# A sparse four-layer graph network: the first table and the output stored by one 128-partition transfer per unit, x in two arrangements, three adjacency blocks loaded earlier

## The chip, the core and the metric

The kernel runs on one core of a Trainium2 chip. The core has a matrix engine (TensorE, PE in the profile, with its weight loads as PEld), VectorE (DVE), ScalarE (ACT), GpSimd (POOL) and SyncE (SP), which only issues transfers. All engines run at the same time, each executes its own instructions in order, and semaphores make one wait for another. Transfers issued by SP and by POOL are carried out by 16 DMA engines. The metric is device time of one execution in microseconds, as the median of several runs; lower is better.

## The reference

The input x has 8 batches of 2048 nodes with 128 features. The adjacency matrix is 2048 by 2048, symmetric, with ones on its diagonal and a random one in about 0.8% of the other places. Four layers follow each other, attention with eight heads (0 and 2) and graph attention (1 and 3):

```python
# layers 0 and 2
Q = (h @ Wq).reshape(B, N, 8, 16); K = ...; V = ...
scores = jnp.einsum('bnhd,bmhd->bhnm', Q, K) / 4
attn = softmax(jnp.where(adj == 0, -inf, scores), axis=-1)
x = layer_norm(h + (einsum('bhnm,bmhd->bnhd', attn, V).reshape(B, N, 128) @ Wo + bo), ln1_g, ln1_b)
x = layer_norm(x + relu(x @ W1 + b1) @ W2 + b2, ln2_g, ln2_b)
# layers 1 and 3
h = x @ W; s_i = h @ a_src; s_j = h @ a_dst
e = leaky_relu(s_i[:, :, None] + s_j[:, None, :], 0.2)
att = softmax(jnp.where(adj == 0, -inf, e), axis=-1)
x = layer_norm(einsum('bij,bjd->bid', att, h) + x) * ln_gamma + ln_beta
```

## The kernel before

The adjacency is sparse, so the kernel (class `Sparse`) makes lists of neighbours first and then works on gathered rows only. A second class, `Dense`, computes everything without lists; it stands in a branch at the end of `net` that is taken only if a list overflowed, which does not occur here.

**Units.** The nodes are cut into 32 units of 64. A unit's data for all 8 batches stands in one tile of 128 partitions and 512 columns: batches are split into two halves of four, the half and the node within the unit together make 128 columns for each of the four batches of a half. Transposed x of a unit, `xt_dram[u]`, has the 128 features on the partitions; its columns run over batch, half, node.

**Setup.** `run` first calls `load` for every fourth unit: one 1 MB transfer brings four units of transposed x into half of a `kv` buffer that serves as a ring. For each unit `project` (with n = 0) multiplies these columns by Wk and Wv (PE, L1404), copies the results into a tile `trows` (ACT or DVE, L1342 and L1344) and stores them into `table_0`, a table in DRAM with one row of 8 KB per node: 4 KB for half 0 (keys of its four batches, then values) and 4 KB for half 1. A unit's tile is thus 128 partitions of 4 KB. With columns in the order half, node, partitions 0 to 63 hold half 0 and partitions 64 to 127 half 1, and `store` (L1459) issues one transfer for each half. `trows` has two buffers, and the setup also uses the one of `hidden`, so three units' rows can be on their way.

`block_list` handles the adjacency in 16 blocks of 128 nodes: a 1 MB load into a `kv` buffer (L1028), a masking pass on DVE (L1036), the search for the 40 largest (L1054, L1067, L1069), positions by small matmuls (L1090). `unit_list` then makes for each of the block's two units (L1111 to L1195) a list of indices `idx` and a one-hot tile `hot`, which ACT converts to one byte an element (`hot8`) and which goes to DRAM as `hots[u]` (L1199, issued on POOL for the first twelve units, on SP after).

**Attention** (`attention`, n = 0 and 2). For each unit `fetch` loads x (L1257) and the one-hot tile (L1268, widened on ACT at L1275), PE computes queries (L1570). Then in five steps POOL gathers the neighbours' table rows (L1536, an indirect transfer of 128 rows; two in four steps, one in the last), PE spreads the queries to them (L1609), DVE multiplies and sums (L1621, L1628), ACT takes exponents (L1638), POOL weighs the values (L1647), PE adds up (L1679). `after_attention` finishes the unit and calls `project` for the next layer's table. A gather waits for the whole table of its layer. **Graph attention** (`graph`, n = 1 and 3) does the same with rows of 1040 floats, 4160 bytes (L1855 to L1893); in layer 3 each unit's result is stored into `out_dram` by `store` (L1958), again one transfer for each half.

**Order.** No engine's order is written by hand. Every operation is recorded as an `Op` with a cost, a key and its reads and writes; `Plan.order` plays the program through with these costs and, on each engine, takes the operation of the smallest key that is ready and finds its buffers free. `in_order` then fixes that order. A key thus says how early an operation may come: loads of x have u - 1500, the first two adjacency blocks i - 1491, the others 10 i - 80, a unit's step in layer n about 1000 n + 5 u. Buffers of a tag such as `kv` (six) are handed out in the order of keys. All plain transfers of SP share eight completion semaphores in turn, and each waits for the transfer eight before it.

Of the kernel before, what the change touches and what calls it, by code (L numbers as in the profile page):

```python
# [9 lines left out]
F32 = mybir.dt.float32  # L10
# [32 lines left out]
QB = 4  # L43
STRIDE = 1000
LEAD = 60

SBUF_BUFS = {
    "kv": 6, "hot": 3, "hot8": 2, "x": 4, "q_sb": 2, "rows": 3, "at": 1, "r": 2, "x1": 2, "hidden": 1, "normed": 2,
# [18 lines left out]
class Dense:  # L67
# [10 lines left out]
    def __init__(self, ctx, tc, x, adj, w, out):  # L78
        self.tc, self.nc, self.w, self.x_in, self.out = tc, tc.nc, w, x, out
        self.B, self.N, _ = x.shape  # L80
        self.NB = self.N // P
        self.NC = self.N // CH

        def pool(name, **kw):
            return ctx.enter_context(tc.tile_pool(name=name, **kw))

        self.const = pool("const", bufs=1)
        self.dram = pool("dram", bufs=1, space=DRAM)
        self.dram2 = pool("dram2", bufs=2, space=DRAM)
        self.ps_s = pool("ps_s", bufs=2, space=PSUM)  # L90
        self.ps_acc = pool("ps_acc", bufs=1, space=PSUM)
        self.ps_m = pool("ps_m", bufs=1, space=PSUM)

        self.constants()
        self.layers = [
            self.mha_weights(n) if kind is MHA else self.gat_weights(n)
            for n, kind in enumerate(LAYERS)
        ]
        self.masks(adj)

        self.one = pool("one", bufs=1)
        self.two = pool("two", bufs=2)
        self.three = pool("three", bufs=3)
        self.four = pool("four", bufs=4)
        self.kpool = pool("kpool", bufs=9)
        self.vpool = pool("vpool", bufs=5)
        self.turn = 0
# [420 lines left out]
    def batch(self, b):  # L528
        x = self.two.tile([P, self.NB, P], F32, name="x")
        self.nc.sync.dma_start(out=x, in_=self.x_in[b].rearrange("(t p) d -> p t d", p=P))  # L530
        for n, kind in enumerate(LAYERS):
            if kind is MHA:
                units = 2 * self.NB * (self.N // QC)
                gen = self.attention(x, n)
            else:
                units = self.NB * self.NC
                gen = self.graph(x, n)
            for u in gen:
                yield u / units
        self.nc.sync.dma_start(out=self.out[:, b, :].rearrange("(t p) d -> p t d", p=P), in_=x)  # L540

    def run(self):

# [211 lines left out]
def flat(ap):  # L755
    return ap if len(ap.shape) == 2 else ap.rearrange("p b d -> p (b d)")


class Sparse:
# [12 lines left out]

    def __init__(self, ctx, tc, x, xt, adj, w, out):
        self.tc, self.nc, self.w, self.xt_in, self.out = tc, tc.nc, w, xt, out
        self.B, self.N, _ = x.shape
        self.NB = self.N // P
        self.NU = self.N // UNIT
        self.HB = self.B // 2  # L780

        def pool(name, **kw):
            return ctx.enter_context(tc.tile_pool(name=name, **kw))

        self.nc.scalar.preload_act_table_set("natural_log_exp_and_others")
        self.const = pool("const", bufs=1)
        self.dram = pool("dram", bufs=1, space=DRAM)
        self.plan = Plan(self.nc)
        self.op, self.cell = self.plan.op, self.plan.cell
        for tag, bufs in SBUF_BUFS.items():  # L790
            self.plan.pool(tag, pool(f"sb_{tag}", bufs=bufs), bufs, tag in BY_KEY)
        for tag, bufs in PSUM_BUFS.items():
            self.plan.pool(tag, pool(f"ps_{tag}", bufs=bufs, space=PSUM), bufs)

        self.constants()
        self.weights_at = [Cell() for _ in LAYERS]
        self.keys_at = Cell()
        self.late = False
        self.whole()
        self.gates = {}  # L800
# [12 lines left out]

        self.xd = self.dram.tile([self.NU, P, CH], F32, name="xd")
        self.x_at = [Cell() for _ in range(self.NU)]
        self.hots = self.dram.tile([self.NU, P, HOT], F8, name="hots")
        self.hots_at = [Cell() for _ in range(self.NU)]
        self.ends_at = [None] * self.NU
        self.t = self.const.tile([P, self.NU, P // GROUP * self.HB], F32, name="t")
        self.t_at = [Cell() for _ in range(self.NU)]  # L820
        self.idx = self.const.tile([P, self.NU, TILES], I32, name="idx")
        self.idx_at = [Cell() for _ in range(self.NU)]


        self.owner = self.const.tile([P, self.NU, TG, 2], F32, name="owner")
        self.ends = self.const.tile([P, self.NU, 2], F32, name="ends")

        self.empty = self.const.tile([P, self.NU, TILES], F32, name="empty")


        self.seen = self.const.tile([P, 4, self.NB], F32, name="seen")
        self.junk = self.const.tile([P, P], F32, name="junk")
        self.stats = self.const.tile([P, 6], F32, name="stats")
        self.eps = self.fixed("eps", EPS)
        self.half = self.fixed("half", 0.5)
        self.rows_n = self.fixed("rows_n", float(self.N))
        self.huge = self.fixed("huge", 1e30)
# [183 lines left out]
    def block_list(self, adj, i):  # L1021
# [5 lines left out]
            {"SP": 0.45},  # L1027
            lambda e: e.dma_start(out=buf.tile[:, 0:N].bitcast(I32), in_=adj[i * P : (i + 1) * P, :]),  # L1028

            i - 1491 if i < 2 else key - 20,  # L1030
            writes=[buf],
            dma=P * N * 4,
        )
# [189 lines left out]
    def load(self, u, ring):  # L1223

        key = u - 1500
        x = Cell()
        at = u % 8 * CH

        def start(e):
            e.dma_start(  # L1230
                out=ring.tile[:, at : at + 4 * CH].rearrange("p (u c) -> p u c", u=4),
                in_=self.xt_in[u : u + 4].rearrange("u p c -> p u c"),
            )

        self.op({"SP": 0.45}, start, key, reads=[self.gates[u - 9]] if u > 8 else [], writes=[x], shares=[ring], dma=4 * P * CH * 4)
        for k in range(4):
            self.project(
                0, u + k, x, key + k, lambda ring=ring, at=at + k * CH: ring.tile[:, at : at + CH], [ring]
            )
# [144 lines left out]
    def project(self, n, u, x, key, of=None, shares=()):  # L1384
# [68 lines left out]
        if halves[-1] == 0:  # L1453
            return

        def store(e):
            for part, nodes, hf in self.parts(u):
                half = hb * width
                e.dma_start(out=self.tables[n][nodes, hf * half : (hf + 1) * half], in_=rows.tile[part])  # L1459

        self.op(
            {"SP": 0.9}, store, key, reads=[rows], joins=[self.table[n]], dma=P * hb * width * 4
        )

    def norm(self, r, key):
# [439 lines left out]
    def after_graph(self, n, u, outs, banks, acc, x, base):  # L1905
# [36 lines left out]
        if n < len(LAYERS) - 1:  # L1942
            x = self.scaled(normed, L["ln_gamma"], L["ln_beta"], "xnew", key)
            self.keep(u, x, key)
            self.project(n + 1, u, x, key)
        else:

            def last(e):
                shape = [P, len(blocks), P]
                e.tensor_tensor(normed.tile, normed.tile, L["ln_gamma"].unsqueeze(1).to_broadcast(shape), ALU.mult)  # L1950
                e.tensor_tensor(normed.tile, normed.tile, L["ln_beta"].unsqueeze(1).to_broadcast(shape), ALU.add)

            op({"POOL": 2.4, "DVE": 1.2}, last, key, writes=[normed], port=True)

            def store(e):
                for part, nodes, hf in self.parts(u):
                    batches = slice(hf * hb + blocks.start, hf * hb + blocks.stop)
                    e.dma_start(  # L1958
                        out=self.out[nodes, batches, :],
                        in_=normed.tile[part],  # L1960
                    )

            op({"SP": 0.9}, store, key, reads=[normed], dma=P * P * 4 * len(blocks))

# [54 lines left out]
        before[i.engine] = i  # L2019


def net(tc, x, xt, adj, w, out):

    with ExitStack() as ctx:
        s = Sparse(ctx, tc, x, xt, adj, w, out)
        s.run(adj)
        count = s.failed()
        in_order(tc)
        failed = tc.nc.values_load(count, min_val=0, max_val=P, skip_runtime_bounds_check_because="a count of partitions")
    with tc.If(failed > 0):  # L2030
        with ExitStack() as ctx:
            Dense(ctx, tc, x, adj, w, out).run()
# [33 lines left out]
```

The softmax here doesn't subtract the row's maximum and nothing guards it: scores larger than these inputs give would overflow.

## Time and profile before

| what | value |
|---|---|
| three runs | 3027.98, 3045.35, 3050.05 us; median 3045.35 |
| profiled execution | span 3033.2 us (its page gives the span alone), mean granted TensorE clock 0.887 |
| busy share of the span | PE 78%, DVE 76%, POOL 70%, PEld 47%, ACT 46% |
| DMA moved | 1022.93 MB, mean 337 GB/s |
| table 0 stores | from 12.7 us to 131.3 us |
| first gather of layer 0, first multiplication | 135.5 us, 176.6 us |
| last addition of layer 0 (PE, L1679) | 1136.9 us |

The page gives each engine's busy time; the windows view gives the same for a stretch of the span; the timeline shows instructions in order with the idle time ahead of them and what ended it; the waits view sums these. "SPq" stands for SyncE's queue, on which an instruction's length is the time that the issue took. Landings are read from the semaphores that a transfer's 16 parts raise, and packet times from the trace's record of every DMA packet.

### The profile page before, as it was taken

To read this page: it belongs to the slowest core of one execution; us is meant where nothing else is said; L and a number is where in the kernel's file an instruction comes from. 1 tells how busy PE (TensorE), PEld (TensorE's weight loads), DVE (VectorE), ACT (ScalarE), POOL (GpSimd) and SP (SyncE) were. 2 spreads that over 40 slices of the span, in tenths; PEclk is the share of its full clock that TensorE was granted. 3 is DMA by queue.
4 is the path that set the end of the run, shared out by engine and by line. 5 is a ranking of instruction groups with operands and counts; after the bars stand their busy time and mean duration, and the time that the engine had idled before them with its cause. 6 is when DMAs were issued, how large, how long until landed. Compare 5 with 4: busy or idle time off the path is not lost. (4 is left out here: it accounts for less than half of the span.)

```text
span 3033.2 us, 60151 instructions
## 1 busy us (share of the span) xinstructions
PE 2358.7 (78%) x22044; PEld 1417.6 (47%) x22044; DVE 2314.6 (76%) x3754; ACT 1405.2 (46%) x4780; POOL 2135.3 (70%) x1454
## 2 busy tenths in 40 slices
PE   6767887788887776787786778878888878677775
PEld 5633444444443334666664234334334334566664
DVE  4779999998887775555553988888987988566665
ACT  4435555455544442555553235445445434344443
POOL 0158886787888873766663878878878875677774
PEclk8768999999999998989988899999999999778777
DMA  8759997988898884999998989989999986899996
GB/s 272 265 200 363 352 350 293 348 321 327 343 344 338 334 314 152 405 407 402 397 405 292 374 327 358 366 341 356 366 361 353 345 337 229 295 400 403 399 396 257
DMA packets 249535, 1022.93 MB, mean 337 GB/s; under 512 B 40272, under 2 KB 54352, under 8 KB 177328
## 3 DMA queue, kind: packets, MB, share of 16 engines
q0 software_dynamic: 166464, 864.44, 73.1%
q1 hardware_dynamic: 82768, 154.56, 14.4%
q8 instruction: 177, 2.90, 0.4%
q14 instruction: 126, 1.03, 0.1%
HBM read 978.59 MB, written 88.08 MB: 352 GB/s over the span
## 5 line engine op out<-in xcount | busy, mean ns | idle before, releaser
L1536 POOL DMA_INDIRECT kv<-table,idx x1152 | 1192.8, 1035 | 645.9 <-issue 291.7
L1647 POOL TENSOR_TENSOR kv<-kv 128x2048 f32<-128x2048 f32 (+1 forms) x259 | 929.4, 3602 | 86.5 <-ACT kv L1638 82.7
L1621 DVE TENSOR_TENSOR kv<-qe,kv 128x2048 f32<-128x2048 f32 (+1 forms) x320 | 662.7, 2071 | 156.2 <-DMA kv<-table,idx 116.6
L1628 DVE TENSOR_REDUCE s<-kv 128x128 f32<-128x2048 f32 (+1 forms) x320 | 660.0, 2062 | 8.1 <-ACT junk L1473 0.5
L1609 PE MATMUL qe<-q_sb,hot 32*128 32x512 f32 (+1 forms) x2304 | 397.2, 693 | 207.5 <-DVE kv L1621 202.0
L1679 PE MATMUL acc<-kv,hot 128*32 128x512 f32 (+1 forms) x2304 | 362.3, 643 | 42.1 <-POOL kv L1647 31.9
L1893 PE MATMUL acc_q<-kv,w 128*32 128x129 f32 (+1 forms) x4608 | 220.1, 326 | 141.6 <-DVE w L1877 113.3
L1609 PEld LDWEIGHTS qe<-q_sb,hot 32*128 32x128 f32 (+1 forms) x2304 | 106.0, 195 | 330.4 <-DVE kv L1621 275.6
L1877 DVE TENSOR_TENSOR w<-hot,e 128x512 f32<-128x512 f32 (+1 forms) x384 | 221.2, 598 | 48.9 <-ACT e L1867 47.7
L1893 PEld LDWEIGHTS acc_q<-kv,w 128*32 128x32 f32 (+1 forms) x4608 | 170.6, 134 | 182.0 <-DVE w L1877 111.2
L1638 ACT ACTIVATE kv<-s 128x128 f32<-128x128 f32 (+1 forms) x320 | 95.0, 297 | 323.1 <-DVE s L1628 172.9
L1855 DVE TENSOR_TENSOR e<-te,kv 128x16 f32<-128x16 f32 (+1 forms) x320 | 58.8, 184 | 237.7 <-DMA kv<-table,idx 234.6
L1473 ACT ACTIVATE junk<-ps_c 128x128 f32<-128x128 f32 x492 | 136.0, 277 | 176.2 <-PE ps_c L1366 151.2
L1342 ACT COPY trows<-ps_p 128x258 f32<-128x258 f32 (+1 forms) x230 | 108.2, 473 | 188.3 <-PE ps_p L1406 93.5
L1867 ACT ACTIVATE e<-e 128x16 f32<-128x16 f32 (+1 forms) x320 | 67.1, 212 | 256.4 <-DVE e L1862 253.4
L1679 PEld LDWEIGHTS sums<-kv,hot 128*32 128x32 f32 (+1 forms) x2304 | 88.6, 118 | 207.3 <-issue 205.1
L1893 PE MATMUL acc<-kv,w 128*32 128x129 f32 (+1 forms) x2304 | 118.8, 307 | 75.2 <-DVE w L1877 69.3
L1366 PE MATMUL ps_c<-centre,r 128*128 128x128 f32 x1008 | 147.6, 291 | 29.7 <-DVE r L1729 18.6
L1376 PE MATMUL ps_f<-x,W 128*128 128x512 f32 (+1 forms) x256 | 151.4, 675 | 17.6 <-ACT x L1516 9.7
L1366 PEld LDWEIGHTS ps_c<-centre,r 128*128 128x128 f32 x1008 | 126.9, 197 | 69.8 <-DVE r L1729 37.0
L1679 PEld LDWEIGHTS acc<-kv,hot 128*32 128x32 f32 (+1 forms) x2304 | 55.1, 114 | 197.2 <-issue 108.6
L1759 PE MATMUL ps_y<-hidden,W 128*128 128x512 f32 (+1 forms) x256 | 142.8, 645 | 4.6 <-ACT hidden L1749 3.0
(205 smaller groups left out, 4028.7 us busy)
## 6 DMA issues: line engine op xcount, KB each, us to landing
table<-trows SPq DMA_DIRECT2D x128, 256.0 KB
x<-xd SPq DMA_DIRECT2D x96, 256.0 KB
xd<-xnew SPq DMA_DIRECT2D x93, 256.0 KB
kv<-table,idx POOLq DMA_INDIRECT x1152
table<-trows SPq DMA_DIRECT2D x128, 130.0 KB
kv<-adj_dram SPq DMA_DIRECT2D x16, 1024.0 KB
kv<-xt_dram SPq DMA_DIRECT2D x8, 1024.0 KB
x<-xt_dram SPq DMA_DIRECT2D x32, 256.0 KB
```

The lines of the kernel that those rows point to most:

```text
L1366: e.matmul(ps.tile[:, cols], lhsT=flat(x.tile)[:, cols], rhs=self.centre, start=True, stop=True)
L1376: lambda e: e.matmul(ps.tile, lhsT=w, rhs=x.tile, start=True, stop=True),
L1473: e.activation(self.junk, x, AF.Square, scale=P**-0.5, accum_out=var.tile[:, b, 1:2])
L1536: e.indirect_dma_start(out=rows(kv.tile, j), out_offset=None, in_=self.tables[n], in_offset=bass.IndirectOffsetOnAxis(ap=self.idx[:, u, co ...
L1609: e.matmul(qe.tile[:, j, hf, :], lhsT=hot.tile[rows, t * P : (t + 1) * P], rhs=q.tile[rows, :], start=True, stop=True,)
L1621: e.tensor_tensor(k, qe.tile[:, 0:tiles].rearrange("p j h c -> p (j h) c"), k, ALU.mult)
L1628: e.tensor_reduce(s.tile[:, 0 : tiles * heads].rearrange("p (q c) -> p q c", q=2 * tiles), k, axis=mybir.AxisListType.X, op=ALU.add,)
L1647: e.tensor_tensor(v, v, w.unsqueeze(3).to_broadcast([P, 2 * tiles, heads // 2, HD]), ALU.mult)
L1679: e.matmul(out[rows, :], lhsT=hot.tile[:, col : col + GROUP * (3 - tiles)], rhs=rhs[:, 2 * j + hf, :], start=(t == 0), stop=(t == TG - 1),)
L1759: lambda e, f=f, ps=ps: e.matmul(ps.tile, lhsT=L["W2"][:, f, :], rhs=hidden.tile[:, f, :], start=(f == 0), stop=(f == FFN // P - 1),),
L1877: e.tensor_tensor(w.tile[:, :, j : j + tiles, :].rearrange("p x j c -> p j x c"), oh[:, j : j + tiles].unsqueeze(2).to_broadcast(shape), e ...
L1893: e.matmul(acc(b)[at : at + GROUP * (3 - tiles), :], lhsT=w.tile[:, hf * hb + b, j : j + 3 - tiles, :].rearrange("p j c -> p (j c)"), rhs= ...
```

## The change

Table 0 and the output get a layout in which a unit's 128 partitions are 128 consecutive rows. For the table this needs a different order of the projected columns, node before half, so that partition 2 t + h holds half h of node t; x is therefore handed over a second time, as `xk_dram`, in this order, and `load` reads it from there. `fetch` still reads `xt_dram`. `out_dram` becomes an array of units, partitions and columns, which the host puts in order. In layer 0 `store` issues one transfer of 128 partitions, and the output likewise; tables 1 to 3 keep two. In the fallback class the output is stored in two parts. The recorded SP cost of these stores goes from 0.9 to 0.45. The first five adjacency blocks get keys of their own.

```diff
+ADJ = (-1499, -1495, -1487, -1479, -1471)
@@ block_list
-            i - 1491 if i < 2 else key - 20,
+            ADJ[i] if i < len(ADJ) else key - 20,
@@ load
-                in_=self.xt_in[u : u + 4].rearrange("u p c -> p u c"),
+                in_=self.xk_in[u : u + 4].rearrange("u p c -> p u c"),
@@ project
+        half = hb * width
+
         def store(e):
+            if n == 0:
+                by_half = self.tables[0].rearrange("n (h c) -> (n h) c", h=2)
+                e.dma_start(out=by_half[u * P : (u + 1) * P, :], in_=rows.tile)
+                return
             for part, nodes, hf in self.parts(u):
-                half = hb * width
                 e.dma_start(out=self.tables[n][nodes, hf * half : (hf + 1) * half], in_=rows.tile[part])
 
         self.op(
-            {"SP": 0.9}, store, key, reads=[rows], joins=[self.table[n]], dma=P * hb * width * 4
+            {"SP": 0.9 if n else 0.45}, store, key, reads=[rows], joins=[self.table[n]], dma=P * half * 4
         )
@@ after_graph
-            def store(e):
-                for part, nodes, hf in self.parts(u):
-                    batches = slice(hf * hb + blocks.start, hf * hb + blocks.stop)
-                    e.dma_start(
-                        out=self.out[nodes, batches, :],
-                        in_=normed.tile[part],
-                    )
-
-            op({"SP": 0.9}, store, key, reads=[normed], dma=P * P * 4 * len(blocks))
+            op(
+                {"SP": 0.45},
+                lambda e: e.dma_start(out=self.out[u][:, cols], in_=flat(normed.tile)),
+                key,
+                reads=[normed],
+                dma=P * P * 4 * len(blocks),
+            )
@@ kernel
-    xt = x.reshape(2, b // 2, n_nodes // UNIT, UNIT, P).transpose(2, 4, 1, 0, 3).reshape(n_nodes // UNIT, P, b * UNIT)
+    parts = x.reshape(2, b // 2, n_nodes // UNIT, UNIT, P)
+    xt = parts.transpose(2, 4, 1, 0, 3).reshape(n_nodes // UNIT, P, b * UNIT)
+    xk = parts.transpose(2, 4, 1, 3, 0).reshape(n_nodes // UNIT, P, b * UNIT)
...
-    out = nc.dram_tensor("out_dram", [n_nodes, b, P], F32, kind="ExternalOutput").ap()
+    out = nc.dram_tensor("out_dram", [n_nodes // UNIT, P, b * UNIT], F32, kind="ExternalOutput").ap()
```

More of the change, by code (lines that the diff above doesn't have):

```diff
@@ L539, in batch @@
                 yield u / units
-        self.nc.sync.dma_start(out=self.out[:, b, :].rearrange("(t p) d -> p t d", p=P), in_=x)
+        halves = P // UNIT
+        out = self.out.rearrange("(t v) (h i) (c d) -> v h c i t d", v=halves, i=UNIT, d=P)
+        for v in range(halves):
+            self.nc.sync.dma_start(
+                out=out[v, b // (self.B // 2), b % (self.B // 2)], in_=x[v * UNIT : (v + 1) * UNIT]
+            )
     def run(self):
@@ L759, with __init__ @@
 class Sparse:
-    def __init__(self, ctx, tc, x, xt, adj, w, out):
-        self.tc, self.nc, self.w, self.xt_in, self.out = tc, tc.nc, w, xt, out
+    def __init__(self, ctx, tc, x, xt, xk, adj, w, out):
+        self.tc, self.nc, self.w, self.xt_in, self.xk_in, self.out = tc, tc.nc, w, xt, xk, out
         self.B, self.N, _ = x.shape
@@ L1953, in after_graph @@
             op({"POOL": 2.4, "DVE": 1.2}, last, key, writes=[normed], port=True)
-            def store(e):
-                for part, nodes, hf in self.parts(u):
-                    batches = slice(hf * hb + blocks.start, hf * hb + blocks.stop)
-                    e.dma_start(
-                        out=self.out[nodes, batches, :],
-                        in_=normed.tile[part],
-                    )
-            op({"SP": 0.9}, store, key, reads=[normed], dma=P * P * 4 * len(blocks))
+            op(
[4 more added lines that the diff above has]
+                dma=P * P * 4 * len(blocks),
+            )
     def run(self, adj):
@@ L2019, in in_order, with net @@
         before[i.engine] = i
-def net(tc, x, xt, adj, w, out):
+def net(tc, x, xt, xk, adj, w, out):
     with ExitStack() as ctx:
-        s = Sparse(ctx, tc, x, xt, adj, w, out)
+        s = Sparse(ctx, tc, x, xt, xk, adj, w, out)
         s.run(adj)
@@ L2050 @@
     b, n_nodes, _ = x.shape
-    xt = x.reshape(2, b // 2, n_nodes // UNIT, UNIT, P).transpose(2, 4, 1, 0, 3).reshape(n_nodes // UNIT, P, b * UNIT)
-    args = [give("x_dram", x), give("xt_dram", xt), give("adj_dram", np.roll(np.asarray(inputs["adj"]), (-FIRST, -FIRST), axis=(0, 1)))]
+    parts = x.reshape(2, b // 2, n_nodes // UNIT, UNIT, P)
+    xt = parts.transpose(2, 4, 1, 0, 3).reshape(n_nodes // UNIT, P, b * UNIT)
+    xk = parts.transpose(2, 4, 1, 3, 0).reshape(n_nodes // UNIT, P, b * UNIT)
+    args = [give("x_dram", x), give("xt_dram", xt), give("xk_dram", xk), give("adj_dram", np.roll(np.asarray(inputs["adj"]), (-FIRST, -FIRST), axis=(0, 1)))]
     weights = []
@@ L2064 @@
     r = run_bass_kernel_spmd(nc, [arrays], core_ids=[0])
-    return np.roll(r.results[0]["out_dram"].transpose(1, 0, 2), FIRST, axis=1)
+    y = r.results[0]["out_dram"].reshape(n_nodes // UNIT, 2, UNIT, b // 2, P)
+    return np.roll(y.transpose(1, 3, 0, 2, 4).reshape(b, n_nodes, P), FIRST, axis=1)
```

## The prediction

> **What bounds the kernel now.** I read the busy shares by stage first (one row per stretch of the trace: its length, then busy time of PE, weight loads, DVE, ACT and POOL with instruction counts, granted TensorE clock, DMA share, GB/s):
> ```profile
> 0.00:134.00 134.00, 99.77 (x421) 82.19 (x421) 78.51 (x262) 57.31 (x136) 9.69 (x37) 0.82 0.82 269
> 134.00:176.00 42.00, 26.32 (x116) 24.22 (x116) 25.69 (x97) 20.21 (x61) 15.46 (x15) 0.50 0.71 282
> 176.00:250.00 74.00, 55.11 (x334) 25.56 (x334) 67.89 (x78) 24.79 (x64) 55.40 (x30) 0.73 0.61 230
> 250.00:1100.00 850.00, 694.19 (x4834) 348.24 (x4826) 753.77 (x819) 430.10 (x1412) 691.60 (x375) 0.93 0.88 334
> 1300.00:1500.00 200.00, 158.69 (x2470) 128.40 (x2470) 105.59 (x368) 107.43 (x378) 131.53 (x129) 0.89 1.02 402
> ```
> From 176 us on layer 0 keeps DVE busy (67.9 of 74, then 753.8 of 850). Layer 1 keeps the DMA engines full (1.02). The first 176 us are full on nothing: DVE has 55 us idle before 134 and 16 between 134 and 176. The change's main edits lie there. So the timeline of this stretch comes next, then its waits:
> ```profile
> 113.75 18.20 SPq L1459 DMA_DIRECT2D table<-trows  x14
> ...
> 135.53 3.10 POOL L1536 DMA_INDIRECT kv<-table,idx  x1 [8.69 <-issue]
> ...
> 148.99 0.62 POOL L1199 DMA_DIRECT2D hots<-hot  x1
> ...
> 165.16 1.00 ACT L1195 ACTIVATE hot<-hot 128x960 fp8e5<-128x960 f32 x1 [4.16 <-DMA hots<-hot]
> ...
> 173.39 1.00 ACT L1275 CAST hot<-hot 128x960 f32<-128x960 fp8e5 x1
> ...
> 174.45 2.09 PE L1609 MATMUL qe<-q_sb,hot 32*128 32x512 f32 x8 [2.56 <-ACT hot L1275]
> ...
> 176.61 2.29 DVE L1621 TENSOR_TENSOR kv<-qe,kv 128x2048 f32<-128x2048 f32 x1 [3.06 <-PE qe L1609]
> ```
> The last store of table 0 is issued at 131.3 and lands at 134.4 by its semaphore; at 135.5 the first gather of it goes out. The first multiplication of layer 0 comes only at 176.6: it waited for a matmul, that for unit 0's one-hot tile (cast at 173.4), and that for a load behind stores of `hots`:
> ```profile
> SPq L1268 <- DMA hots<-hot: 33.4, 1, 33.4
> ```
> is the SP queue's longest single wait before 300 us. Before 134 us the copies into `trows` waited for earlier stores to land (total, times, longest):
> ```profile
> ACT trows L1342 <- DMA table<-trows: 13.8, 7, 4.1
> ...
> DVE trows L1344 <- DMA table<-trows: 12.8, 2, 7.7
> ```
>
> [...] among stores alone (100 to 134 us) the 4 KB packets split into about 160 and 307 to 382 ns, mean 230; in layer 1, among gathers, such packets take 161. [...] A pair issued at 118.3 and 118.9 begins to land at 121.0 and 121.8. [...] The `hots` store of 148.99, behind nine gathers on POOL's queue, held ACT until 165.16. [...] The row 134 to 176 shows 0.50; ten list matmuls (L1145) take 2.43 us there and 1.24 at 56 us (clock 0.92).
>
> **The change, part by part.** "First multiply" is the 176.6 us above; the order of instructions is read from the two built programs.
>
> *Stores of table 0.* 64 SP issues of 256 KB (0.45 to 0.60 us each) become 32 of 512 KB. A unit's rows come free when both halves have landed, about 0.65 us earlier without the second issue; nine waits x 0.65 = 6 us. The packets, 1408, 1278 and 1410 of them in the three stretches to 134 us at 195, 193 and 230 ns, would take 160: 190 us over 16 engines, 12 us of DMA time. DMA is not full here (0.82), so I take little of that: last landing -7 us, bounds 0 and -18 (6 + 12).
>
> *x in a second arrangement.* The same eight 1 MB loads; later fetches of x still read the old one. 0.
>
> *Adjacency earlier.* Both programs load eight blocks before attention begins; three move from 61 to 80 us to between the x loads. Each is 1 MB, 128 packets of 8 KB at about 350 ns: 2.8 us of the rings. Two of them now stand ahead of the second and third x load. Those landed at 9.5 and 12.2, and would land near 12.3 and 17.8; PE is busy with the first four units until about 17.3, so this is hidden, and if projections caught up it would cost 3 us. DVE gets about 16 us more list work before the last projection (85 against 69, counted by durations), into its 55 us idle. On PE the lists of two more units (about 2.4 us each) and not one query product (2.07) stand before the last projection: +2.7 us on the last landing.
>
> *Hand-over.* Between last projection and first query spread PE had three blocks' offsets, seven unit selections and the parts of five units; now one, two and two, and a query. At half clock: 3.3 + 2 x 0.65 + 2.07 + 2 x 2.9 + 2.1 for the spread = 14.6 us. Alongside, the gathers: 1.1 to the first issue, 4.4 for two, some 5 for 2 MB, 10.5. The first load of unit 0's one-hot tile now waits only for `hots` stores that stand ahead of every gather on POOL, so the 33 us wait goes. First multiply 16 us after the last landing, where it was 42.2; bounds 11 (gathers alone) and 30. What is late next is PE's list work at half clock.
>
> *What is deferred.* At the first multiply nine units' lists are done, not eleven. Two x 2.33 us of DVE (L1167 to L1179) come in layer 0, where DVE is full: +4.7. Eight `trows` copies move from DVE to ACT (8 x 0.69 us), in a stretch where DVE idles: 0. On SP the ninth adjacency load now stands between the one-hot loads of units 0 and 1 and waits for the first gather's buffer. Unit 1's tile is queued behind it and then loads beside gathers; unit 0's five steps (about 21 us) cover most: +3, bounds 0 and 8.
>
> *Output.* 62 stores of 128 KB become 31 of 256, the last four become two. Packets stay 2 KB (84 ns) and bytes are equal, so layer 3's full DMA gains nothing; SP waits there for DVE, so 31 issues saved hide. At the end SP reads the count at 3019.68, 0.3 us after the others, but PE's branch lasts until 3024.4: 0.
>
> *Rest of layer 0.* The same instructions in another order (one row weighting moves from DVE to POOL); from layer 1 on PE, DVE, ACT and POOL have an identical order. 0, bounds -8 and +8.
>
> Sum: last landing 134.4 - 7 + 2.7 = 130; first multiply 146, 30.6 earlier; + 4.7 + 3 = **-23 us**. Against the profiled span of 3033.2 that is 3010. The page gives no time around the span; the three runs are 3027.98, 3045.35 and 3050.05, so their median is 12 us above it and 5 below their highest. I subtract from the median: **3022**.
>
> **The rivals.**
> *The start stays late.* The stores free nothing, because PE (99.8 of 134 busy at clock 0.82) sets the last landing, and first multiply comes 30 us after it, since the lists drag at half clock. 134.4 + 2.7 + 30 = 167, 9.5 earlier; + 4.7 + 3 leaves -2: 3043. For it: PE is the busiest engine before 134. Against: the gaps behind store landings.
> *The stores were the bound.* All 18 us come through: 134.4 - 18 + 2.7 + 16 = 135, 41.5 earlier; + 7.7 gives -34: 3011. For it: 26.6 us of waits on landings, DMA at 0.82; against: SP often waits for ACT's copies (38.7 us before 300), not for DMA.
> *Slower: layer 0's new order.* Where DVE is full (176 to 1100), the remaining eight blocks' list work falls at other places between multiplications. If it comes before a multiplication whose successor on PE or POOL then starves, each unit pays; 1 us a unit is +32, less the 23: 3055. It decides from 0.75 us a unit. For it: DVE idles only 96 of 850 us, PE and POOL are at 82%. Against: the amount of work is equal.
> That the change is not in the program is excluded by the built order.
>
> **Numbers.** Forecast 0.5, start stays late 0.2, stores the bound 0.2, slower 0.1. The forecast's bounds, all at one end at once, would give 2995 or 3059; as independent (root of the squares: 11, 5, 3, 8 below; 7, 3, 14, 5, 8 above) they give 3007 to 3041, its own range. The favourable rival with layer 0's -8 gives 3003, and measurement adds some 10 either way (runs of before spread 22). Range 2990 to 3050, leaving out most of the slower case and the outer tails. One per cent, 30 us, is about what this measurement can tell from no change. Faster by more (below 3015): 0.15 from the forecast's lower part, 0.15 from the second rival, 0.02 else = 0.32. Slower by more (above 3076): 0.06 from layer 0's order at nearly 2 us a unit. Within: 0.62.
>
> **What would show it.** Stores: 32 issues for table 0, their 4 KB packets near 160 ns, copy waits on landings well under 26 us. Last landing at 125 to 133 us; after 140 the stores step is wrong. First multiply at 140 to 152 with no long SP wait on a `hots` store; near 165 the hand-over step is wrong. Layer 0's last multiplication and everything after should shift by one constant; a growing shift is the third rival. The tail after the last DVE instruction stays near 14 us.

## The result, and the profile after

The changed kernel takes 3027.34 us (median of 20 runs, 3010.68 to 3037.61), the kernel before 3033.82 us beside it (20 runs, 3023.67 to 3050.05). Where the two were timed in turn the ratio is 0.9965, 95% interval 0.9947 to 0.9982: about 10.6 us faster, between 5 and 16. The forecast was 23 us, a ratio of 0.9924, which lies outside that interval. That the forecast 3022 lies near the measured number has another reason: it was taken off 3045.35, the median of three runs, and that of twenty is 11.5 us lower. So the direction was right and the gain about half.

The profiled execution of the changed kernel is the longest of its 20 runs (3037.61 us, a span of 3035.9, clock 0.882); before had a span of 3033.2. Spans of single executions say little here; stages do, and even these only where several executions agree. The busy shares by stage, with the columns of the prediction:

```profile
0.00:134.00 134.00, 104.99 (x454) 86.29 (x454) 92.05 (x329) 71.53 (x170) 12.92 (x41) 0.82 0.75 273
134.00:176.00 42.00, 36.20 (x207) 23.84 (x206) 30.98 (x37) 18.02 (x53) 28.86 (x20) 0.61 0.88 349
176.00:250.00 74.00, 52.44 (x346) 25.77 (x347) 63.33 (x79) 29.56 (x93) 55.94 (x32) 0.84 0.80 301
250.00:1100.00 850.00, 694.57 (x4694) 349.75 (x4693) 731.74 (x802) 419.39 (x1379) 677.96 (x365) 0.91 0.86 325
```

In the setup DVE is busier (92.1 us against 78.5), and from 134 to 176 us POOL works 28.9 us against 15.5: layer 0 is already running. But from 176 to 250 us DVE works 63.3 against 67.9, and from 250 to 1100 us 731.7 against 753.8. What was won early is lost in the two lower rows, on the engine that is fullest there.

The timeline of the hand-over, all engines, changed kernel:

```profile
111.86 15.40 SPq L1467 DMA_DIRECT2D table<-trows  x7
...
130.84 1.08 POOL L1547 DMA_INDIRECT kv<-table,idx  x1 [13.49 <-DVE cand L1075]
...
134.64 0.99 ACT L1281 CAST hot<-hot 128x960 f32<-128x960 fp8e5 x1
...
138.87 2.09 PE L1620 MATMUL qe<-q_sb,hot 32*128 32x512 f32 x8
...
141.03 2.29 DVE L1632 TENSOR_TENSOR kv<-qe,kv 128x2048 f32<-128x2048 f32 x1 [0.87 <-PE qe L1620]
```

The last store of table 0 lands at 129.7 by its semaphore (before 134.4), the first gather goes out at 130.84 (135.53), unit 0's one-hot tile is cast at 134.6 (173.4), and the first multiplication comes at 141.0 (176.6): 35.6 us earlier. SP's waits before 300 us (total, times, longest):

```profile
SPq L1034 <- DMA kv<-table,idx: 23.3, 2, 12.9
...
SPq L1274 <- DMA hots<-hot: 14.3, 2, 13.7
```

The wait of 33.4 us ahead of unit 0's one-hot tile is gone; the 13.7 us for `hots` come later, ahead of the third one-hot load (172.3 us). New is a wait of the ninth adjacency load for a gather's buffer. The copies' wait for landed stores before 140 us:

```profile
ACT trows L1348 <- DMA table<-trows: 16.7, 5, 5.5
```

That is all of it now; before it was 13.8 on ACT and 12.8 on DVE. The 4 KB packets of the stores take 164, 182 and 168 ns in the three stretches up to 134 us (195, 193 and 230 before; the forecast's 160 for all of them was an estimate from the shorter ones of before), and 32 issues do what 64 did.

Then the waits of DVE from 180 to 1130 us, first before, then after:

```profile
DVE kv L1621 <- DMA kv<-table,idx: 48.8, 36, 3.7
DVE kv L1621 <- PE qe L1609: 10.7, 10, 1.9
...
DVE r L1729 <- PE ps_o L1376: 7.3, 1, 7.3
```

```profile
DVE kv L1632 <- DMA kv<-table,idx: 42.5, 24, 5.1
DVE kv L1632 <- PE qe L1620: 25.9, 16, 9.1
DVE r L1740 <- PE ps_o L1382: 16.3, 7, 7.2
```

DVE waits less for gathers and more for PE: 15 us more for spread queries, 9 more for the output projection. In all these two come to 25.9 and 16.3 us here; E2 and E12, which have this order too, have 19.4 and 16.8, and 15.1 and 18.4. Layer 0 from its first multiplication to its last took 970.8 us before and 1004.6 in this execution; of the lead of 35.6 us 1.7 were left at its end.

### The profile page after: what moved, and what is told of

It is laid out like the page before. It is cut to its first block, busy times and chain, and to the rows that moved or that the text cites. A ratio compares the mean times of both kernels' runs of the same rounds, so it can differ in the third digit from the quotient of the medians.

```text
span 3035.9 us, 60069 instructions
## 1 busy us (share of the span) xinstructions
PE 2383.0 (78%) x22044; PEld 1429.6 (47%) x22044; DVE 2306.6 (76%) x3744; ACT 1409.6 (46%) x4789; POOL 2139.0 (70%) x1455
## 5 line engine op out<-in xcount | busy, mean ns | idle before, releaser
L1690 PE MATMUL acc<-kv,hot 128*32 128x512 f32 (+1 forms) x2304 | 372.6, 660 | 60.0 <-POOL kv L1658 43.9
L1904 PEld LDWEIGHTS acc_q<-kv,w 128*32 128x32 f32 (+1 forms) x4608 | 171.5, 135 | 172.3 <-DVE w L1888 100.1
L1484 ACT ACTIVATE junk<-ps_c 128x128 f32<-128x128 f32 x492 | 136.1, 277 | 162.8 <-PE ps_c L1372 137.0
L1348 ACT COPY trows<-ps_p 128x512 f32<-128x512 f32 (+1 forms) x238 | 113.3, 478 | 190.1 <-PE ps_p L1412 102.0
L1372 PE MATMUL ps_c<-centre,r 128*128 128x128 f32 x1008 | 150.8, 295 | 28.8 <-DVE r L1740 18.4
L1372 PEld LDWEIGHTS ps_c<-centre,r 128*128 128x128 f32 x1008 | 130.1, 201 | 73.2 <-DVE r L1740 36.7
```

The lines of the kernel that those rows point to most:

```text
L1372: e.matmul(ps.tile[:, cols], lhsT=flat(x.tile)[:, cols], rhs=self.centre, start=True, stop=True)
L1484: e.activation(self.junk, x, AF.Square, scale=P**-0.5, accum_out=var.tile[:, b, 1:2])
L1690: e.matmul(out[rows, :], lhsT=hot.tile[:, col : col + GROUP * (3 - tiles)], rhs=rhs[:, 2 * j + hf, :], start=(t == 0), stop=(t == TG - 1),)
L1904: e.matmul(acc(b)[at : at + GROUP * (3 - tiles), :], lhsT=w.tile[:, hf * hb + b, j : j + 3 - tiles, :].rearrange("p j c -> p (j c)"), rhs= ...
```

## Experiments

Every kernel's order of instructions could be fixed apart from its transfers, so the change splits cleanly: stores (with x twice), output, and order (adjacency keys with the recorded cost). The times of the stages, from one profiled execution each, in us; "layer 0" runs from its first multiplication (L1621) to its last, "rest" from there to the end of the span; the ratio is to the kernel before, with its interval.

| kernel | first gather | first mult. | last mult. | layer 0 | rest | ratio |
|---|---|---|---|---|---|---|
| before | 135.5 | 176.6 | 1147.4 | 970.8 | 1885.8 | 1 |
| the change | 130.8 | 141.0 | 1145.7 | 1004.6 | 1890.2 | 0.9965 [0.9947, 0.9982] |
| E1 stores, old order | 121.2 | 161.6 | 1129.5 | 967.8 | 1877.5 | 0.9973 [0.9959, 0.9987] |
| E2 order, old stores | 135.1 | 144.7 | 1141.1 | 996.4 | 1876.6 | 0.9999 [0.9986, 1.0012] |
| E3 output alone | 136.1 | 177.2 | 1143.4 | 966.2 | 1876.9 | 0.9987 [0.9966, 1.0008] |
| E4 change without output | 131.1 | 141.3 | 1132.8 | 991.5 | 1886.7 | 0.9960 [0.9946, 0.9975] |
| E5 E1, one-hot stores on SP | 129.1 | 169.5 | 1148.1 | 978.7 | 1879.3 | 0.9966 [0.9950, 0.9981] |
| E6 before, one-hot stores on SP | 132.8 | 172.6 | 1155.9 | 983.2 | 1887.2 | 0.9999 [0.9977, 1.0020] |
| E7 E4, one load moved | 130.1 | 140.3 | 1123.4 | 983.1 | 1892.5 | 0.9969 [0.9953, 0.9985] |
| E8 E4, one-hot stores on SP | 129.3 | 139.6 | 1137.9 | 998.3 | 1888.0 | 0.9967 [0.9950, 0.9983] |
| E9 E4, second gather late | 132.6 | 158.6 | 1153.7 | 995.0 | 1894.6 | 1.0024 [1.0006, 1.0043] |
| E10 stores and cost | 118.6 | 157.2 | 1153.7 | 996.5 | 1893.8 | 1.0028 [1.0012, 1.0043] |
| E11 stores and output, old order | 126.4 | 166.9 | 1137.2 | 970.3 | 1886.1 | 0.9966 [0.9949, 0.9982] |
| E12 the change again | 130.9 | 141.1 | 1133.0 | 991.9 | 1887.4 | 0.9973 [0.9955, 0.9991] |

One thousandth of the ratio is 3 us.

### E1: the stores alone

```diff
-                in_=self.xt_in[u : u + 4].rearrange("u p c -> p u c"),
+                in_=self.xk_in[u : u + 4].rearrange("u p c -> p u c"),
...
+            if n == 0:
+                by_half = self.tables[0].rearrange("n (h c) -> (n h) c", h=2)
+                e.dma_start(out=by_half[u * P : (u + 1) * P, :], in_=rows.tile)
+                return
```

> Only the transfers of table 0 change: x in the second arrangement, one 128-partition store a unit; keys and recorded costs are those of before, so that every engine has the order of before. The output is as before. FORECAST (store packets gain, hand-over gains separately): last landing of table 0 about 7 us earlier, near 127; the one-hot tile of unit 0 is still late behind stores of hots on POOL's queue, so the first multiplication moves by no more than those 7 us (168 to 172); total -3 to -8 us, ratio 0.997 to 0.999. If STORES WERE THE BOUND: last landing near 116 to 118, total -15 or more. If LAYER 0 ABSORBS any earlier start: first multiplication 168 to 172 all the same, the shift gone by the end of layer 0, total 0 +-3.

8 us faster (4 to 12). The profiled execution is the shortest of its 22 runs (3008.70 us, median 3022.28). In it the last store lands at 120.1, 14.3 us earlier, which is more than forecast; the first multiplication comes 15.0 earlier, still 40 us after the gather. So the stores shorten the setup and do nothing for the hand-over. Whether the shorter packets or the halved number of issues does it was not separated. Nothing is absorbed: the shift is 15.0 at layer 0's first multiplication and 17.9 at its last. DVE's waits on PE in layer 0 (180 to 1130 us) stay small:

```profile
DVE kv L1626 <- PE qe L1614: 9.0, 10, 1.7
...
DVE r L1734 <- PE ps_o L1376: 2.3, 2, 2.1
```

### E2: the order alone

```diff
-            i - 1491 if i < 2 else key - 20,
+            ADJ[i] if i < len(ADJ) else key - 20,
...
-            {"SP": 0.9}, store, key, reads=[rows], joins=[self.table[n]], dma=P * hb * width * 4
+            {"SP": 0.9 if n else 0.45}, store, key, reads=[rows], joins=[self.table[n]], dma=P * hb * width * 4
```

> Only the order of the change: adjacency keys and recorded SP cost 0.45 for table 0, so that PE, DVE, ACT and POOL have the order of the changed kernel; the stores stay two of 64 partitions, x and the output as before. FORECAST with GIVING BACK IN LAYER 0: first multiplication 5 to 8 us later than in the changed kernel, at 146 to 150 (hand-over gains about 28), then a shrinking lead in layer 0 as in the changed kernel, nothing left at its end or a loss; total -5 to +5. If the ORDER ALONE makes the gain: -8 to -11 as the changed kernel, ratio 0.996. If the slower rival (layer 0's new order) holds in full: +5 or more.

No gain (-4 to +4 us), although the first multiplication comes 31.9 us earlier. The last store lands at 133.8 (before 134.4), so three more blocks among the loads of x cost nothing there. Layer 0 takes 996.4 us where it took 970.8, and 25.6 of the 31.9 us are gone at its end. The hand-over's gain and layer 0's loss both come with these two lines, the adjacency keys and the cost; E10 takes them apart.

### E3 and E4: the output

```diff
             def store(e):
-                for part, nodes, hf in self.parts(u):
...
+                e.dma_start(out=self.out[u][:, cols], in_=flat(normed.tile))
```

> Only the output: one 128-partition transfer a unit and block of columns into the new layout, recorded cost left at 0.9, so that every engine has the order of before. FORECAST: 0 +-2, layers 0 to 2 unchanged, the tail after the last DVE instruction near 14 us. If the OUTPUT makes the gain (fewer issues on SP[...]): -6 to -11 us, all of it in layer 3 and the tail.

E4 is the changed kernel with the old `store` of the output put back.

> The change without its output edit: table 0 by one store a unit, x twice, costs and adjacency keys; PE, DVE, ACT and POOL have the order of the changed kernel. FORECAST: same as the changed kernel within 2 us, ratio 0.996 to 0.997, first multiplication near 141, the lead shrinking through layer 0 in the same units as in the changed kernel's trace (if it is the order that stalls) or in other units (if it is the variation of one execution). If the OUTPUT makes the gain: within 2 us of before.

The output alone gives -10 to +2 us, which decides nothing; but the change without it (-12, interval -16 to -8) is not measurably slower than the change. So the output is no part of the gain that can be seen; a gain of a few us is not excluded. E4's lead in layer 0 shrinks from 35.3 to 14.6 us in the same units as in the change: unit 0's stretch, from its first multiplication to unit 1's, takes 33.8 and 33.6 us (before 25.6), unit 5's 35.9 and 36.7 (28.2), unit 12's 45.9 and 45.9 (34.7); unit 10's, shorter in both, 29.0 and 29.0 (40.6, but 36.6 to 40.6 among the executions with the old order). It is the order, not the execution.

### E5 and E6: the one-hot stores off POOL's queue

```diff
-            lambda e: e.dma_start(out=self.hots[u], in_=hot8.tile),
+            lambda e: (self.nc.sync if 6 <= u < LEAD // TG else e).dma_start(out=self.hots[u], in_=hot8.tile),
```

> E1 (table 0 by one store a unit, order of before) with one thing more: the one-hot stores of units 6 to 11 are issued by SP in place of POOL, so that they no longer stand behind the gathers on POOL's queue. PE, DVE and ACT keep the order of before, POOL too but for these six issues. First gather near 121 as in E1, first multiplication near 142 to 148 (in E1 161.6), about where the changed kernel has it. If it is LAYER 0'S NEW ORDER that gives the lead back (my theory): here the order is the old one, the lead of some 30 us at the first multiplication is still there at layer 0's last (shift -25 to -35), total -20 to -30, ratio 0.990 to 0.993. If LAYER 0 ABSORBS an earlier start whatever its order (gathers, throttle): the lead shrinks to about -15 by its end, total as E1, -8 +-4.

> The kernel before with only the one-hot stores of units 6 to 11 on SP in place of POOL; two stores a unit, old x, keys, costs. First gather at 135 as before, first multiplication near 156 to 162 (before 176.6). LAYER 0'S NEW ORDER as the loser: lead of 15 to 20 us carried to the end of layer 0, total -12 to -20, ratio 0.993 to 0.996. LAYER 0 ABSORBS: 0 to -5.

E5 has the edits of E1 as well, E6 no others. They were to bring the early start without the new order, and didn't: the first multiplication comes at 169.5 and 172.6, 40 us after the first gather as before. In E5 SP's longest wait is now for ACT (before 300 us):

```profile
SPq L1199 <- ACT hot L1195: 86.1, 9, 32.3
```

ACT's timeline shows why:

```profile
138.01 1.01 ACT L1195 ACTIVATE hot<-hot 128x960 fp8e5<-128x960 f32 x1
...
141.00 1.01 ACT L1195 ACTIVATE hot<-hot 128x960 fp8e5<-128x960 f32 x1
...
166.28 1.01 ACT L1275 CAST hot<-hot 128x960 f32<-128x960 fp8e5 x1
```

In the old order the seventh and eighth list are converted 10 and 13 us after the last landing, whatever queue carries their stores: here at 138 and 141 us (landing 128.0), in E1 at 130 and 133 (landing 120.1). SP stands at the first of these stores until 139, with the load of unit 0's tile behind it; the load goes at 150.0, and its cast stands behind one more conversion on ACT, at 165.4. The queue was one link of that chain; taking it out showed the next. E5's total is that of E1. Whether the old order of layer 0 would keep a lead of 30 us was not tried in another way.

E5 shows something else. Up to the last store it has the order of E1, and E11 has it too, but the last store lands at 120.1 in E1, 125.3 in E11 and 128.0 in E5. The stretch from 40 to 50 us, E1 and then E5:

```profile
40.00:50.00 10.00, 9.68 (x48) 8.21 (x48) 4.15 (x8) 4.15 (x11) 0.75 (x1) 0.83 0.82 294
```

```profile
40.00:50.00 10.00, 9.62 (x35) 8.69 (x36) 3.60 (x8) 2.75 (x7) 0.00 (x0) 0.51 0.61 210
```

PE is busy for the whole stretch in both, but at a clock of 0.83 it finishes 48 matmuls and at 0.51 only 35. Just ahead a copy on ACT had waited 0.38 us for a store's landing in E1 and 1.91 in E5. In E11 it waited 1.97, and the clock of the stretch is 0.55. That the longer gap let the clock fall is a guess; no run tested it alone. One execution thus sizes the setup to no better than 8 us.

### E7 and E8: what lengthens unit 0

E7 holds back one transfer:

```diff
+            if i == 8:
+                self.late = go      # the ninth adjacency load
+            else:
+                go()
...
-                lambda e: e.dma_start(out=hot8.tile, in_=self.hots[u]),
+                lambda e: (e.dma_start(out=hot8.tile, in_=self.hots[u]), self.late() if n == 0 and u == 1 else None),
```

> E4 (the change without its output edit) with one transfer moved on SP: the ninth adjacency load goes behind the one-hot load of unit 1 in place of ahead of it; everything else has the order of E4. In E4 unit 0's stretch (first multiplication of unit 0 to that of unit 1) takes 33.8 us, before 25.6. If THIS SP ROW costs what the stretch grew by: stretch 26 to 29, total 5 to 8 us below E4. If the DEFERRED LISTS cost it (PE's list matmuls ahead of the query spread, ACT waiting for a one-hot store behind gathers): stretch 32 to 34, total within 3 us of E4.

E8 is E4 with the edit of E5, from unit 8 on.

> E4 with the one-hot stores of units 8 to 11 issued by SP in place of POOL. In E4 ACT waits 4.5 us at 166.6 for such a store behind gathers, and the cast of unit 1's tile stands behind that. On SP the stores of units 8 and 9 now stand ahead of the ninth adjacency load. If that wait on ACT is what lengthens unit 0: stretch 26 to 30 in place of 33.8, total -4 to -8 below E4. If the DEFERRED LISTS themselves (DVE and PE time, order of PE) do: stretch 32 to 34, and the losses of later units (5, 12, 17) as in E4; total within 3 us of E4, well above E5.

With the load moved, unit 0's stretch is 33.1 us (E4 33.8) and the total no lower than E4's: the SP row costs nothing that can be seen. (In its one profile E7 has a layer 0 of 983.1 us, 8 below E4's; the totals don't show such a gain.) E8 makes the stretch longer (37.2) and the total no lower. That leaves the work itself that now lies in unit 0. In E4 its timeline shows how it counts:

```profile
150.08 2.27 PE L1146 MATMUL ps_l<-unit_aux,hot 128*128 128x86 f32 x10
...
152.14 0.49 PE L1153 MATMUL ps_l<-unit_aux,hot 128*128 128x1 f32 x2
...
152.56 2.09 PE L1615 MATMUL qe<-q_sb,hot 32*128 32x512 f32 x8
152.67 0.57 DVE L1168 TENSOR_TENSOR pick<-rank,ps_l 128x400 f32<-128x400 f16 x1 [1.45 <-PE ps_l L1153]
...
154.72 2.29 DVE L1627 TENSOR_TENSOR kv<-qe,kv 128x2048 f32<-128x2048 f32 x1 [0.87 <-PE qe L1615]
...
159.32 0.29 DVE L986 COPY Wt<-ps_w 128x128 f32<-128x128 f32 x1 [1.37 <-PE ps_w L985]
...
162.73 0.16 DVE L998 COPY Wx<-ps_wa 128x1 f32<-128x1 f32 x1 [0.93 <-PE ps_wa L989]
```

DVE pays for a list not only with its own passes. PE's selections stand ahead of the query spread that the next multiplication needs, so DVE waits 1.45 us for them, and 0.87 for the spread behind them. A second list in the same unit costs 2.51 us of waiting at 171.9. And not only lists were deferred: the last two lines prepare a weight of the next layer (`Wt`, `Wx`), for which DVE waits 1.37 and 0.93 us. In the old order this lies ahead of the first multiplication (at 134 and 150 us in the kernel before), where DVE does not wait for it; the prediction has no term for it.

### E9: has layer 0 a pace of its own?

```diff
             for j in range(tiles):
                 col = 2 * t + j
+                if n == 0 and u == 0 and col == 1:
+                    for _ in range(10):
+                        e.memset(rows(kv.tile, 1), 0.0)
```

> E4 (the change without its output edit) with ten clears of 128x2048 words on POOL between the first and the second gather of layer 0, some 19 us by the 1.85 us of a 128x2048 pass on POOL at the start of the trace before; every engine keeps the order of E4. The first multiplication moves from 141 to some 160, where E1 has it. If LAYER 0 HAS A PACE OF ITS OWN that takes up an earlier or later start: its last multiplication moves by less than 8 us and the total by 0 to +8 against E4 (ratio to before 0.996 to 0.999). If its NEW ORDER loses the time and the start is carried through (my theory): the last multiplication 15 to 20 us later than in E4, total +15 to +20 against E4, slower than before by 3 to 10 us.

POOL's timeline has the delay where it was put:

```profile
132.60 1.07 POOL L1545 DMA_INDIRECT kv<-table,idx  x1 [13.49 <-DVE cand L1070]
133.67 18.58 POOL L1544 MEMSET kv<- 128x2048 f32 x10
152.52 1.03 POOL L1545 DMA_INDIRECT kv<-table,idx  x1 [0.27 <-POOL kv L1544]
```

Against E4 the first multiplication is 17.3 us later, that of unit 10 17.8, of unit 22 17.7, the last 20.9; the total rises from 0.9960 to 1.0024, some 19 us (by the two intervals 12 to 27). A start of layer 0 counts in full. The rival that it takes up any shift is out, and so is the thought that the loss is something that an early start brings about: with a late start and the same order it is the same.

### E10: a third order

Table 0's one store and the recorded cost, with the old adjacency keys.

> Table 0 by one store a unit with its recorded SP cost of 0.45, adjacency keys of before: a third order, which neither the kernel before nor the changed one has. It too leaves one unit's list more to layer 0 (ten done ahead of the first multiplication of DVE's order, against eleven before and ten in the change). If DEFERRED LISTS cost layer 0 its time: layer 0 from its first to its last multiplication 985 to 1000 us as in the changed kernel (983 to 1005), against 971 before, total near before. If the loss belongs to the PARTICULAR ORDER that the adjacency keys give: 965 to 985, total -8 to -15.

Layer 0 takes 996.5 us again and the kernel is 8 us slower than before, though its first multiplication comes 19.5 us earlier. Here it is another wait that grew most (24.4 us on ACT's copies of layer 1's rows, 6.8 before). So the loss does not need the adjacency keys: two orders that leave a list more to layer 0 lose some 27 us each against the old one's 969. (Ahead of the first multiplication DVE has eleven lists done in the old order, ten in E10, and in the change nine and the first two passes of a tenth.) The early hand-over does need the keys: in E10 the first multiplication comes 39.7 us after the last landing (117.5), about as late as before (42.2). The keys with the old cost, which might have the one without the other, were not run. For the total I had expected a draw with the kernel before. With two such orders the number of lists and the placement of the rest can't be told apart.

### E11 and E12: the change without its order, and the change

E11 joins the edits of E1 and E3.

> The change without its reordering: table 0 and the output by one store a unit, x twice, but recorded cost 0.9 and the adjacency keys of before, so that every engine has the order of before. If the transfers make the whole gain: -8 to -13, the same as the changed kernel beside it within 4 us. If the ORDER adds to it: the changed kernel is 4 us or more below this one. If the OUTPUT gains too: this one is 3 to 4 us below E1, -11 to -13.

> The changed kernel once more, beside E11 on the same chip. -8 to -13 against before. Its profile: first multiplication within 2 us of 141, the stretches of units 0, 5, 12 and 17 again 4 us or more above those of before (the losses are of the order, not of one execution); a last multiplication of layer 0 at 1145.7 again would make the first profile typical, one near 1130 an execution that lost more than most.

E11 and the change are the same within their intervals (0.9966 and 0.9973). The reordering brings nothing in sum. E12's profile has the first multiplication at 141.1, unit 0 at 33.8, unit 5 at 38.1, unit 12 at 44.8 and unit 17 at 39.4 us (31.4 before), and the last at 1133.0: the first profile of the change lost more than most. No version was measurably better than the change; E4, the lowest, overlaps it.

E11 and E12 have the same transfers and differ in the order alone. Layer 0 in E11 and then in E12, from the first multiplication to the last, with the columns of the prediction (DVE's is the third busy time):

```profile
166.88:1137.21 970.33, 785.47 (x5424) 393.71 (x5428) 863.95 (x930) 476.49 (x1552) 776.88 (x420) 0.92 0.85 324
```

```profile
141.14:1133.02 991.88, 797.09 (x5429) 401.52 (x5430) 863.21 (x943) 480.50 (x1566) 791.93 (x427) 0.91 0.86 326
```

DVE works as long in both (864.0 and 863.2 us), and the 21.6 us between them are idle time. They are lost by the start of unit 20 (E12 is 23.6 us longer up to there), in whose stretch the last list is finished in both; after that nothing more is lost. So the loss falls where lists are still placed between the units. Not every wait is behind list work, though. The longest one in E12:

```profile
723.65 0.99 ACT L1281 CAST hot<-hot 128x960 f32<-128x960 fp8e5 x1 [5.34 <-DMA hot<-hots]
...
726.01 0.58 ACT L1348 COPY at<-ps_t 128x512 f32<-128x512 f32 x1
...
728.25 2.07 PE L1382 MATMUL ps_o<-at,Wo 128*128 128x512 f32 x2
...
730.36 0.75 DVE L1740 SCALAR_TENSOR_TENSOR r<-ps_o,bo,x 128x512 f32<-128x512 f32 x1 [7.90 <-PE ps_o L1382]
```

DVE waits 7.90 us for an output projection whose input `at` ACT copies only at 726.0, because ACT had stood 5.34 us for a one-hot load. PE runs no list work in this time.

## Why the prediction was right in direction and more than twice too large

*Stores of table 0, -7 on the last landing.* Right within its bounds (0 to -18): 6.4, 9.1 and 14.3 us in three executions of the old order, 4.1 in the new (E2 to the change: 133.8 to 129.7). The old stores vary too: 131.7 us in E6, 134.9 in E3. In total they give 8 us (E1), which is nearly the whole gain.

*Adjacency earlier, +2.7.* Between nothing (E2, 133.8 against 134.4) and 10 us (129.7 in the change against 120.1 to 128.0 with the stores alone). The sum of this term and the last, 130, was measured as 129.7 (128.2 to 131.4 in the other executions with both edits); that doesn't confirm the two terms one by one.

*Hand-over, 16 us after the last landing.* 11.3, at the favourable bound, so that the first multiplication came at 141.0 and not 146. The reason given was only half of it: the `hots` stores behind gathers on POOL's queue were not what set the late start alone. E5 took them off that queue and the start stayed late; it needed the order that the adjacency keys give (E2; E10 without them starts late).

*What is deferred, +4.7 on DVE and +3 on SP, and the rest of layer 0 at 0, within 8.* Here the prediction failed, in size. The four executions with the old order on every engine (before, E1, E3, E11) have layer 0 at 966.2 to 970.8 us, mean 968.8; the five with the new one and no transfer moved (the change, E2, E4, E9, E12) at 991.5 to 1004.6, mean 995.9. The terms together are +27, not +7.7. The executions that moved transfers are less far apart: E5 and E6 have 978.7 and 983.2 with the old order on PE, DVE and ACT, E7 and E8 983.1 and 998.3 with the new; with them the means differ by 22.

Of the 27 us DVE works 2.6 (860.8 us in the mean of the four, 863.4 of the five), less than the 4.7 for the deferred lists, and the SP row is nothing (E7). The other 24.5 are idle time of DVE, for which the prediction had only the term of 0: it took the other blocks' work as neutral because its amount is equal. Its place isn't: one unit gains 11.6 us (unit 10), another loses 11.2 (unit 12). In unit 0 the traces show the idle time behind PE's selections and behind a weight that is prepared there; at the longest wait, behind a late one-hot load on ACT. How the rest divides was not shown.

The clock is a rival that no run sets apart. Over layer 0 the granted TensorE clock is 0.92 in the four and 0.90 to 0.91 in the five, and a slower PE may have lengthened DVE's waits, or the waits have lowered the clock; neither was shown. It is not the whole: unit 0 has 0.63 before and 0.61 in the change, and 25.6 and 33.6 us; unit 16 has 0.98 and 0.74, and 33.3 and 32.6 us.

With the measured terms the sum comes out: 35.6 us at the first multiplication less 27 leaves 8 to 9; the two measurements of the change give 10.6 and 8.2. The parts from layer 1 on range over 10 us among the six executions with the old order and over 18 among the seven with the new, with means of 1882 and 1888; a loss of a few us there is not excluded. *Output, 0*: nothing seen. *Tail near 14 us*: 13.9 after DVE's last instruction.

*The rivals.* "The start stays late" and "the stores were the bound" are both refuted, by 141.0 and by 129.7. "Slower: layer 0's new order" named the right place. It had PE or POOL starve behind DVE's list work; what the traces show is that DVE's own waits grew, in this order mostly those for PE. (Its forecast is 3022 + 32, thus 3054, and 23 us over 32 units are 0.72 each; the prediction rounds both up.) Beyond the 7.7 us of the forecast it cost 19 us, or 0.6 us a unit, below the 0.75 from which it would have turned the sign; in E10, which lacks the early hand-over, it did turn it. The sign that the prediction named for it, a lead that changes through layer 0 in place of a constant one, is what the trace shows.

*Open:* which placements of list work cost what, and whether an order exists that starts at 141 us and takes 969 us for layer 0. That would be worth the 27 us that this one loses. The adjacency keys with the old cost are the nearest that was not run.

## What to carry to other kernels

Work pushed out of an idle setup into a full stage was not priced here by its own duration on the full engine (2.6 us more work of DVE, 24.5 us more idle time): add what it puts ahead of the next operand on the engines that feed it, and look at which unit each piece lands in. An earlier start and a longer stage can be one edit (here 35.6 us earlier and 27 longer), so time the stage from its own first instruction to its last, and split a change into what its transfers do and what its order does; here the transfers were the whole gain. And take the forecast off a median of many runs, or state it as a ratio: three runs were off by as much as the change is worth.

## What the runs showed that was not expected

The setup's length is not fixed by the program: with the same order on every engine up to there, the last store lands anywhere from 120.1 to 128.0 us, and the executions part near 40 us, where one runs PE at a clock of 0.83 and another at 0.51.

In the changed kernel a masking pass of DVE (L1042, 128x2048), 2.28 us by itself, took 7.44 us when it began at 561.67 us beside two value weightings of POOL that ran from 561.38 for 5.58 us: it ended 2.16 us after them. All seven passes that were lengthened in before, the change, E1 and E12 ended 2.15 to 2.16 us after such a weighting. It goes the other way too: a pass of 2.23 us at 443.47 was not lengthened, and the weighting that began 0.08 us after it took 5.68 us in place of 3.68. Such passes lie in the old order as well (one of 6.55 us), so they don't explain the difference between the two.
